# Projections of two batches from 49 products in two levels, with weight sums streamed from DRAM

## The chip, the cores and the metric

The kernel runs on one core of a Trainium2 chip. The metric is the device time of one execution in microseconds (us), as the median of several runs. All arithmetic is in fp32.

## What is computed

The input x is 64 batches of 256 nodes with 512 features, and a 256 x 256 adjacency matrix that all batches share. Two layers follow, each with a residual. Cut to what matters:

```python
h = relu(layernorm(x))                       # layer 0: graph attention
Wh = h @ W
logits = leaky_relu((Wh @ a_src)[:, :, None] + (Wh @ a_dst)[:, None, :], 0.2)
x = x + softmax(where(adj, logits, -inf)) @ Wh
h = relu(layernorm(x))                       # layer 1: 8 heads of 64
q, k, v = (split_heads(h @ M.T + b) for M, b in ((Wq, bq), (Wk, bk), (Wv, bv)))
a = softmax(where(adj, q @ k.T / 8, -inf)) @ v
x = x + merge_heads(a) @ Wo.T + bo
```

## The kernel before

**Tiling.** A group is one batch (GB = 1): 256 tokens in two halves of 128, 512 features in four chunks of 128. There are 64 groups. Each large product of 256 x 512 by 512 x 512 (or 256 x 256 by 256 x 512) is cut into two by two quarters and made from seven products of quarters in place of eight (a Strassen-Winograd form). `chained` (L624) holds it: seven terms, each a quarter or a sum of quarters of the left operand with a quarter or a sum of the right one. The products are summed in three PSUM banks, a, b and d: after every product the bank's running sum is read out and put, or added, to the quarters of the result that want it (`assemble`, L646).

**Stages.** In layer 0, `normalize0` (L960) makes h and the node terms, `weights0` (L1011) the edge weights em and the reciprocals rb of their sums, `quarters0` (L1057) scales em by rb and makes the sums of quarters of h and em on POOL, `aggregate0` (L1087) the product of em and h in 7 products of two 128-column matmuls, `transform0` (L1185) the product with W in 7 products of two 256-column matmuls, added to x. In layer 1, `normalize1` (L1192) and `transpose1` (L1220) make hT: VectorE transposes blocks of 32, and a trip through DRAM (z to rows to hT) does the rest. `project_qk` (L1263) makes queries and keys of one group in 7 products of eight 128-column matmuls, `project_v` (L1302) the values in 7 products of two 256-column matmuls. `attention` (L1325) makes the scores of four head pairs (arrays of 64 rows), exponentials on ScalarE, mask products and sums over the nodes on VectorE, the values product (arrays of 64 columns), and head sums `psm` in arrays of 32 columns (`head_sums`, L1373), whose reciprocal rc goes through DRAM to be spread over partitions (row, rb). `scale` (L1427) applies it; `output` (L1447) is the product with Wo in 7 products, added to x and stored. All weights and their sums lie in SBUF (`load_quarters`, L588; `combine_w`, L600).

**What sets the order.** The stages are generators. A list written out by hand (`first_half`, `second_half`) says in which order their steps are recorded. A planner (`Plan`) then orders the instructions: it gives each a duration (`cost`, L402), PE's steps a rank from the table `PHASE`, where one unit is one group, and plays the engines forward. PE takes the first step among the next AHEAD = 22 by rank that can start and for which PSUM banks are free; the other engines take what is due first. A chain of products reserves three of the eight banks. The order that comes out is issued as it stands, each engine a queue in order; SP issues nearly all DMAs. The planner's `Engine` issues everything, so the profile gives nearly every instruction the line L384; the tiles tell them apart.

**Names.** pqk_a, pqk_b, pqk_d: the banks of `project_qk`; pv: values; po: `transform0` with w_sb and `output` with wo_sb; pu: aggregate; psc: scores; pav: values product; psm: head sums; ps: edge sums; hs, us, as, hq, eq: sums of quarters; ex: exponentials; sm: their sums; va: values' left quarter, unpacked. The general path after the flag is not taken.

Of the kernel before, what the change touches and what calls it, by code (L numbers as in the profile page):

```python
# [30 lines left out]
class Buffer:  # L31

    def __init__(self, pool, shape, dtype, tag, name, bufs, real=None):
        self.pool, self.shape, self.dtype, self.tag, self.name = pool, shape, dtype, tag, name
        self.bufs, self.real = bufs, real
        self.grain = 32 if math.prod(shape[1:]) >= 256 else 1
        self.reads, self.writes, self.ops = [], [], []
        self.before = self.bank = self.chain = None

# [91 lines left out]
class Pool:  # L131
# [3 lines left out]
    def tile(self, shape, dtype, tag, name, bufs=None):  # L135
        base = Buffer(self.pool, shape, dtype, tag, name, bufs or self.bufs)
        made = self.made.setdefault(tag, [])
        if len(made) >= base.bufs:
            base.before = made[-base.bufs]
# [4 lines left out]
class Op:  # L144
# [12 lines left out]
AHEAD = 22  # L157
SLACK = 6.67358
SPARE = 1.08917
STEADY = 1  # L160
PHASE = {
    "aggregate0": [-1.42646, -1.3706, -1.36386, -1.35194, -1.33305, -1.33142, -1.3049, -1.30085],
    "attention": [0.44654, 0.6298, 0.47698, 0.36017, 0.40555, 1.35722],
    "output": [1.56205, 1.65037, 1.65572, 1.69495, 1.72281, 1.85231, 1.89845],
    "project_qk": [0.31881, 0.32614, 0.34745, 0.36874, 0.37077, 0.44626, 0.51693],
    "project_v": [0.62352, 0.64711, 0.66878, 0.71995, 0.81445, 0.83399, 0.9563],
    "transform0": [-0.55259, -0.50904, -0.48995, -0.48575, -0.45644, -0.44964, -0.39606],
    "weights0": [-1.61854, -1.58152, -1.43348],
}
8  # L170
# [3 lines left out]
class Plan:  # L174
# [16 lines left out]
    def record(self, engine, method, args, kwargs):  # L191
# [3 lines left out]
        for write, views in ((False, op.ins), (True, op.outs)):  # L195
            for v in views:
                base, bits = v.base, v.area()
                if write and base.before is not None:
                    for o in base.before.ops:
                        op.deps[o.at] = o  # L200
# [23 lines left out]
    def deadlines(self, slack):  # L224

        for n, block in enumerate(self.blocks):
            block.rank = n - len(self.blocks)
            if block.label is not None:
                stage, g, k = block.label
                block.rank = g + PHASE[stage][min(k, len(PHASE[stage]) - 1)]  # L230
# [18 lines left out]
    def schedule(self, ahead, slack):  # L249
# [60 lines left out]
        while len(order) < total:  # L310
# [12 lines left out]
            if free["tensor"] <= now:  # L323
                open_banks = [n for n, t in enumerate(bank_free) if t <= now]
                for n, block in enumerate(blocks[:ahead]):
# [11 lines left out]
                    for base in new.values():  # L337
                        if base.chain is not None:
                            if base.chain in reserved:
                                others -= reserved[base.chain]  # L340
                            else:
                                need = 3
                    if len(open_banks) < need + others:
                        continue
                    for base in new.values():
# [3 lines left out]
                        if base.chain is not None:  # L349
                            reserved[base.chain] = reserved.get(base.chain, 3) - 1  # L350
# [3 lines left out]
                    for op in block:  # L354
                        if op.kind != tile_kind:
                            t += 0.09 if tile_kind == (P, P) else 0.17
# [45 lines left out]
def cost(op):  # L402
# [15 lines left out]
    elif op.engine == "tensor":  # L418
        left = op.args[1]
        size = [next(s for s in (32, 64, 128) if k <= s) for k in (left.shape[0], left.size)]  # L420
        op.step = {512: 0.858, 256: 0.432, 128: 0.2245, 64: 0.24}.get(n, 0.11)
# [41 lines left out]
def kernel(  # L463
# [54 lines left out]
    half = const.tile([P, 2, Q], F32, tag="half", name="half")  # L518
    nc.gpsimd.memset(half, 0.0)
    for r in range(2):  # L520
        nc.gpsimd.memset(half[:, r, r * (Q // 2) : (r + 1) * (Q // 2)], 1.0)
# [44 lines left out]
    const_tiles = dict(ident=ident, ones=ones, half=half, minus_half=minus_half, bo_b=bo_b, flag=flag)  # L566

    def bounded(plan):
# [6 lines left out]
        ident, ones, half, minus_half, bo_b, flag = (  # L575
            plan.wrap(const_tiles[nm]) for nm in ("ident", "ones", "half", "minus_half", "bo_b", "flag")
# [44 lines left out]
        CHAIN = ((0, "a"), (2, "b"), (1, "a"), (4, "d"), (3, "a"), (6, "d"), (5, "a"))  # L621
        CHAIN_V = ((0, "a"), (1, "a"), (2, "b"), (4, "d"), (3, "a"), (6, "d"), (5, "a"))

        def chained(a, s, name, product, read, order=CHAIN):  # L624

            terms = (
                (partial(a, 0, 0), B11),
                (s[:, 1], T2),
                (partial(a, 0, 1), B21),
                (s[:, 2], T3),  # L630
                (s[:, 0], T1),
                (partial(a, 1, 1), T4N),
# [3 lines left out]
            for n, key in order:  # L636
                left, slot = terms[n]
                left = left() if callable(left) else left
                first = key not in banks
                if first:  # L640
                    banks[key] = bank([P, D], f"{name}_{key}", name)
                product(banks[key], left, slot, first)
# [20 lines left out]
        def product_rows(wt, dst, left, slot, first):  # L663
            for c in range(2):
                nc.tensor.matmul(
                    dst[:, 0:HD], left[:, c], wt[:, slot, c, :],
                    start=first and c == 0, stop=c == 1, skip_group_check=not first,
                )

        def product_cols(wts, dst, left, slot, first):  # L670
            for n, wt in enumerate(wts):
                for e in range(2):
                    at = (2 * n + e) * P
                    for c in range(2):
                        nc.tensor.matmul(
                            dst[:, at : at + P], wt[:, slot, c, e * P : (e + 1) * P], left[:, c],
                            start=first and at == 0 and c == 0, stop=c == 1,
                            skip_group_check=True,
                        )
# [16 lines left out]
        for i, tag in enumerate(("hT", "xn")):  # L696
            w_c.append(big.tile([P, 2, D], F32, tag=tag, name=f"w_{tag}", bufs=2 if tag == "hT" else 1))
# [6 lines left out]
        wq_sb = load_quarters(wqT, "wq_sb")  # L704
        wk_sb = load_quarters(wkT, "wk_sb")
        load_group(2)
        w_sb = load_quarters(w, "w_sb")
        wv_sb = load_quarters(wvT, "wv_sb")
# [4 lines left out]

# [60 lines left out]

        def whole(wt):

            return ((wt[:, B11], wt[:, T3]), (wt[:, B21], wt[:, B22]))
# [22 lines left out]
        def value_squares():  # L800

            for n, slot in enumerate((B11, B21, B22, T3)):
                junk = work.tile([P, DC // 2, HD], F32, tag="ex", name=f"junk_v_{n}", bufs=4)
                nc.scalar.activation(
                    junk, wv_sb[:, slot], AF.Square, accum_out=svs[:, n : n + 1]
                )
# [989 lines left out]
```

## Time and profile before

| what | value |
|---|---|
| median of 3 runs | 2823.18 us (2822.07 to 2823.32) |
| profiled execution, own time | 2824.94 us |
| its span, first to last instruction | 2823.2 us |
| mean granted TensorE clock | 0.999 |
| DMA | 184.49 MB, mean 65 GB/s |

The profile is one execution. PE is TensorE's matmuls, PEld its weight loads (beside PE), DVE VectorE, ACT ScalarE, POOL GpSimd, SP the engine that issues DMAs. A group row has the line, the engine, the operation, output and inputs by tile name, shapes, the count, then busy time and the mean of one, then the idle time of the engine just ahead of these instructions and what ended it. A timeline row has start and length in us, then the instructions merged. Ends of matmuls are modelled, so the pace is read from starts. An fp32 matmul leaves two records.

### The profile page before, as it was taken

The numbers are of one execution on the slowest core, as the hardware profiler recorded it, in microseconds if no ns is written. First come the engines' busy times: TensorE is split into PE (matmuls) and PEld (weight loads), VectorE is DVE, ScalarE is ACT, GpSimd is POOL, SyncE is SP. The second block draws the span as 40 slices with busy tenths as digits, with TensorE's granted clock in tenths as the row PEclk, the third lists the DMA queues.
The fourth block names the chain that finished last, engine by engine and source line by source line (L and its number), as shares of the span: only waits on it lengthen the run. The fifth ranks groups of instructions, "written<-read, shape, count | busy, mean of one in ns | idle before, by whom it ended". The sixth has DMA issues, their size and how long they took to land.

```text
span 2823.2 us, 52681 instructions
## 1 busy us (share of the span) xinstructions
PE 2799.1 (99%) x19698; PEld 2403.9 (85%) x19698; DVE 1838.9 (65%) x3314; ACT 1509.1 (53%) x3974; POOL 1528.7 (54%) x2020
## 2 busy tenths in 40 slices
PE   8999999999999999999999999999999999999999
PEld 5888888888888888888888888888888888888886
DVE  6776666666666666666666666665666666666654
ACT  5645655555555555555555555555555555555532
POOL 4645546556565555465565655554645656555540
PEclk9999999999999999999999999999999999999999
DMA  4022212122122222121221221211212212122120
GB/s 142 27 64 78 68 51 74 55 70 75 47 80 70 65 63 65 55 72 51 76 65 56 79 68 61 69 59 61 72 50 78 64 56 80 60 68 70 57 68 24
DMA packets 124074, 184.49 MB, mean 65 GB/s; under 512 B 28657, under 2 KB 74020, under 8 KB 123814
## 3 DMA queue, kind: packets, MB, share of 16 engines
q1 hardware_dynamic: 123718, 181.05, 20.4%
q8 instruction: 159, 2.61, 0.4%
q14 instruction: 101, 0.83, 0.1%
q0 software_dynamic: 96, 0.01, 0.0%
HBM read 106.44 MB, written 66.57 MB: 61 GB/s over the span
## 4 chain that ended last, share of the span: by engine, by line
PE 97%; ACT 1%; DVE 1%; DMA 0%; issue 0%; POOL 0%; SPq 0%; ACTq 0%
PE pqk_a L384 16%; PE po_a L384 15%; PE psc L384 9%; PE pqk_d L384 8%; PE pav L384 8%; PE pv_a L384 8%; PE po_d L384 8%; PE pqk_b L384 4%; PE pu_a L384 4%; PE pv_d L384 4%; PE po_b L384 4%; PE psm L384 2%; PE pv_b L384 2%; PE pu_d L384 2%; PE pu_b L384 1%; PE ps L384 1%
## 5 line engine op out<-in xcount | busy, mean ns | idle before, releaser
L384 DVE TENSOR_TENSOR ex<-ex,maskT 128x512 f32<-128x512 f32 x512 | 393.8, 800 | 95.0 <-ACT ex L384 95.0
L384 ACT ACTIVATE qk<-pqk_a,bias 128x128 f32<-128x128 f32 x756 | 221.1, 367 | 437.4 <-PE pqk_a L384 437.4
L384 POOL TENSOR_TENSOR em<-em,rb 128x256 f32<-128x256 f32 x122 | 120.1, 997 | 378.6 <-DVE rb L384 377.0
L384 ACT ACTIVATE ex<-psc 128x512 f32<-128x512 f32 x512 | 261.6, 617 | 117.0 <-PE psc L384 117.0
L384 POOL TENSOR_TENSOR as<-aT 128x256 f32<-128x256 f32 x62 | 64.7, 1044 | 423.2 <-PE pqk_a L384 271.0
L384 DVE TENSOR_TENSOR x<-po_a,x 128x256 f32<-128x256 f32 x500 | 205.1, 411 | 100.7 <-PE po_a L384 96.9
L384 PE MATMUL psc<-qk 64*128 64x256 f32 x2048 | 254.3, 389 | 2.1
L384 DVE SCALAR_TENSOR_TENSOR junk<-wa,h 128x512 f32<-128x512 f32 x252 | 183.3, 728 | 81.3 <-ACT h L384 76.6
L384 PE MATMUL pav<-ex,v 128*64 128x256 f32 x2048 | 236.0, 382 | 0.0
L384 DVE RECIPROCAL rc<-psm 128x256 f32<-128x256 f32 x64 | 112.4, 1756 | 185.9 <-PE psm L384 185.9
L384 PEld LDWEIGHTS psc<-qk 64*128 64x128 f32 x2048 | 187.2, 186 | 50.7 <-ACT qk L384 18.2
L384 DVE TENSOR_TENSOR sm<-ex 128x512 f32<-128x512 f32 x256 | 211.7, 828 | 0.0
L384 PEld LDWEIGHTS pav<-ex,v 128*64 128x64 f32 x2048 | 141.0, 137 | 81.8 <-issue 8.7
L384 POOL TENSOR_TENSOR x<-x,bo_b 128x512 f32<-128x512 f32 x128 | 172.2, 1358 | 63.7 <-ACT xn L384 61.5
L384 ACT ACTIVATE h<-x,nmr,rstd 128x512 f32<-128x512 f32 x128 | 101.1, 810 | 127.2 <-POOL nmr L384 127.2
L384 POOL TENSOR_TENSOR hq<-h 128x256 f32<-128x256 f32 x122 | 90.4, 742 | 122.3 <-PE pu_d L384 121.9
L384 ACT COPY v<-pv_a 128x256 f32<-128x256 f32 x192 | 70.6, 368 | 137.8 <-PE pv_a L384 134.8
L384 POOL TENSOR_TENSOR hs<-hT 128x256 f32<-128x256 f32 x128 | 100.4, 806 | 75.0 <-PE pv_d L384 64.2
L384 POOL TENSOR_TENSOR us<-uT 128x256 f32<-128x256 f32 x126 | 106.8, 866 | 61.9 <-DVE uT L384 61.8
L384 PE MATMUL pqk_d<-hs,wq_sb 128*128 128x128 f32 x1008 | 135.4, 277 | 0.0
L384 PE MATMUL po_a<-w_sb,uT 128*128 128x256 f32 x504 | 133.7, 388 | 0.5 <-DVE x L384 0.5
L384 PE MATMUL pqk_a<-hs,wq_sb 128*128 128x128 f32 x1008 | 133.2, 275 | 0.0
(229 smaller groups left out, 7373.4 us busy)
## 6 DMA issues: line engine op xcount, KB each, us to landing
x<-in_x_dram SPq DMA_DIRECT2D x64, 512.0 KB
out_dram<-x SPq DMA_DIRECT2D x128, 256.0 KB
rows<-z SPq DMA_DIRECT2D x62, 512.0 KB
hT<-rows SPq DMA_DIRECT2D x248, 128.0 KB
rb<-row SPq DMA_DIRECT2D x124, 256.0 KB
es_b<-es_b SPq DMA_DIRECT2D x61, 127.0 KB
row<-rc SPq DMA_DIRECT2D x124, 4.0 KB
es_b<-es SPq DMA_DIRECT2D x122, 0.5 KB
```

Of the source, the lines that this page charges most:

```text
L384: getattr(getattr(self.nc, op.engine), op.method)(*map(real, op.args), **{k: real(a) for k, a in op.kwargs.items()})
```

## The change

**Projections.** `project_qk` and `project_v` go; `project(g)` makes queries, keys and values of two groups, g and g + 1, together. The left operand is now 512 tokens by 512 features, cut two by two with one group as each row of quarters, and each of the 7 products of this level is again made from 7: 49 products, each of a 128 x 256 by 256 x 128 shape with its inner 256 in two slots. Their matmuls are three of 128 columns for queries, keys and values. In the outer level the sums of the left operand, S, are made on POOL; in the inner level their halves' sums are made on VectorE (`half_sums`). After each of the 49 products a read of 384 columns (three times 128) takes the bank's running sum: eight are copies with bias on ScalarE, 41 are adds on VectorE into a tile `total` or one of four result tiles c; two sums of such tiles (`add_up`) are on POOL.

**Weight sums from DRAM.** The 49 right operands no longer fit: `weight_products` makes them during the first pair (subtractions on VectorE, copies on ScalarE) into chunks, which are used and stored to a DRAM tensor `products`. Each later pair loads them again in 28 DMAs of up to 128 x 768 values, through four buffers `wst`, on SP.

**Chains.** All chains use two banks, a and b; product 4 starts bank b anew. A chain reserves two banks in the planner.

**Reciprocals.** In `weights0` the edge sums come out with one column a half (`ps` of 128 x 2), their reciprocal is of two columns, two transposes spread it over 256 columns of PSUM (`prs`), and VectorE scales em by it, a step that POOL did in `quarters0`. In `head_sums`, for all but the last two groups, the 256 columns are folded into 64: 32 matmuls of 64 columns with `eighths` in place of 8 of 256, then a reciprocal of 64 columns and three DMAs in place of four.

**Order.** The hand-written list goes. Stages are recorded pair after pair, each score step, values step and head sum a step of its own, and the table `PHASE` has one row for even and one for odd groups, interpolated over a stage's steps (STEPS); AHEAD is 9. The unit is still one group. hT is unpacked by ScalarE into `left` in one copy a half, so `va` goes. The first group is projected through the same 49 products as the others.

The core of the diff:

```diff
-AHEAD = 22
-SLACK = 6.67358
+AHEAD = 9
+SLACK = 3.38563
+STEPS = {"project": 49, "transform0": 7, "output": 7, "aggregate0": 8}
 PHASE = {
+    "project0": [-0.08576, 0.2165, 0.52314, 0.90716, 1.04988, 1.47497, 1.83359, 2.09944],
+    "attention0": [0.75994, 0.85786, 1.51533, 1.51841, 1.68258, 1.67665, 1.79903],
+    "attention1": [2.13243, 2.11902, 2.3234, 2.30657, 2.53841, 2.54761, 2.50817],
+    "output0": [2.11483, 2.51629, 2.65299],
+    "output1": [3.16977, 3.36346, 3.50541],
+    "weights00": [-1.67184],
...
-                                need = 3
+                                need = 2
...
-        CHAIN = ((0, "a"), (2, "b"), (1, "a"), (4, "d"), (3, "a"), (6, "d"), (5, "a"))
+        CHAIN = ((0, "a"), (2, "b"), (1, "a"), (4, "b"), (3, "a"), (6, "b"), (5, "a"))
+        FIRST = (0, 2, 4)
...
+            sums(nc.gpsimd, [S[:, m] for m in range(4)], a)
+            for n in ORDER:
+                if n in groups:
+                    x, name, members = groups[n]
+                    s = half_sums(x, name)
...
+                for slots in CHUNKS:
+                    chunk = chunk_of(f"wst_{g}_{n}_{slots[0]}")
...
+                    if g == 0:
+                        weight_products(n, chunks, slots)
+                        both = both[1], both[0]
+                    nc.sync.dma_start(*both)
+                banks = {}
+                for l, key in CHAIN:
+                    if key not in banks:
+                        banks[key] = bank([P, D], f"pp_{g}_{n}_{key}", f"pp_{g}_{n}")
+                    ps, first = banks[key], l in FIRST
+                    for m in range(3):
+                        pair = chunks[l][:, m], terms[l]
+                        nc.tensor.matmul(
+                            ps[:, m * P : (m + 1) * P], *(pair if m < 2 else reversed(pair)),
+                            start=first and m == 0, stop=True, skip_group_check=True,
                         )
+                    read(n, l, ps)
+                    yield
...
+            if g:
+                prs = bank([P, N], f"prs_{g}")
+                for t in range(NT):
+                    nc.tensor.transpose(
+                        prs[:, t * P : (t + 1) * P], rs[:, t : t + 1].to_broadcast([P, P]), ident
+                    )
+                nc.vector.tensor_mul(em, em, prs.unsqueeze(1).to_broadcast([P, NC, N]))
...
-                for m in range(NC):
-                    nc.gpsimd.tensor_tensor(em[:, m, :], em[:, m, :], rb, op=ALU.mult)
...
+                psm = bank([P, N // parts], f"psm_{g}")
+                rc = work.tile([P, N // parts], F32, tag="rc", name=f"rc_{g}")
                 for r in range(2):
+                    for c in range(parts):
+                        at = Q - (parts * r + c + 1) * (Q // (2 * parts))
+                        for e in range(DC):
+                            nc.tensor.matmul(
+                                psm[e * Q : (e + 1) * Q, :],
+                                ones_at[:, at : at + Q],
+                                sums[e][:, r, c * (N // parts) : (c + 1) * (N // parts)],
+                                start=(r == 0 and c == 0),
+                                stop=(r == 1 and c == parts - 1),
+                            )
                 nc.vector.reciprocal(rc, psm)
```

## The prediction

> **What bounds the kernel now.** I read the page's head and the chain that ended last first: they say which engine sets the end.
>
> ```profile
> span 2823.2 us, 52681 instructions
> ## 1 busy us (share of the span) xinstructions
> PE 2799.1 (99%) x19698; PEld 2403.9 (85%) x19698; DVE 1838.9 (65%) x3314; ACT 1509.1 (53%) x3974; POOL 1528.7 (54%) x2020
> ...
> PE 97%; ACT 1%; DVE 1%; DMA 0%; issue 0%; POOL 0%; SPq 0%; ACTq 0%
> ```
>
> TensorE is busy 99% of the span and carries 97% of the chain. A busy PE isn't yet a PE at its peak, so I read the windows next, over nine groups at a time (columns: length, then busy time and instructions of each engine).
>
> ```profile
> 541.20:930.30 389.10, 388.77 (x2756) 337.28 (x2756) 254.52 (x460) 211.54 (x558) 217.12 (x288) 1.00 0.21 65
> 930.30:1319.40 389.10, 388.77 (x2756) 337.27 (x2755) 254.60 (x460) 211.53 (x558) 217.11 (x288) 1.00 0.21 65
> ```
>
> The two stretches are alike: 389.1/9 = 43.23 us a group, DVE 28.3, ACT 23.5, POOL 24.1 of it. Two groups, a pair, cost 86.5 us. Then the timeline of PE, for the pace (from one start to the next; every fp32 matmul leaves two records).
>
> ```profile
> 1428.99 1.03 PE L384 MATMUL pv_a<-wv_sb,va 128*128 128x256 f32 x4
> 1429.95 3.67 PE L384 MATMUL pav<-ex,v 128*64 128x256 f32 x32
> 1433.55 1.07 PE L384 MATMUL psm<-sm,half 128*32 128x256 f32 x16
> 1434.55 1.13 PE L384 MATMUL po_a<-w_sb,uT 128*128 128x256 f32 x4
> 1435.52 1.03 PE L384 MATMUL po_b<-w_sb,uT 128*128 128x256 f32 x4
> 1436.38 1.03 PE L384 MATMUL po_d<-w_sb,us 128*128 128x256 f32 x4
> ...
> 1443.41 1.05 PE L384 MATMUL pqk_a<-hs,wq_sb 128*128 128x128 f32 x8
> 1444.30 1.06 PE L384 MATMUL pqk_a<-hs,wk_sb 128*128 128x128 f32 x8
> ```
>
> Eight records of 128 columns take 0.893 us (0.2233 a matmul), four of 256 take 0.864 (0.432 a matmul): 1.69 to 1.74 ns a column, so a saved column is saved time. A change of array shape costs 0.10 going in and up to 0.20 coming out (psm to po_a to po_b: 0.14 + 0.10 over the bare pace). A group is 56 matmuls of 128 for queries and keys (12.50), 14 of 256 for values (6.05), 28 for the two transforms (12.10), 14 of 128 for the aggregate (3.11), scores and values 3.46 each, head sums 0.86, edge sums 0.43: 41.97. The remaining 1.25 us are shape changes, three visits to the narrow shapes a group. No wait is left in it.
>
> **What the Trainium skill says.** "TensorE: Matmul & The Clock Gate", section "Back-to-back issue gap", gives matmuls of 1 to 64 columns a floor of about 25 ns each. The trace before has 64-column work only in the Gram products, at (23.17 to 24.16)/32 = 31 ns a record with the shape change in it: it shows nothing faster, though there only two array parts work side by side and streaming alone would give 27. "TensorEngine Tiling (Array Packing)", section "Key Properties", says that a change of tiling mode drains the array; the 0.10 to 0.20 us above agree. "SBUF — State Buffer", section "Who interferes with whom", says that a DVE instruction with two SBUF inputs contends with a POOL instruction that reads SBUF, one with a single SBUF input doesn't. The trace agrees: the mask product (two SBUF inputs) runs 648 to 1694 ns, the add from PSUM of po_d 405 to 426.
>
> **The change, part by part, for a pair.** The rows of DVE that the costs come from:
>
> ```profile
> L384 DVE TENSOR_TENSOR x<-po_d,x 128x256 f32<-128x256 f32 x250 | 104.7, 419 | 36.0 <-PE po_d L384 33.7
> L384 DVE TENSOR_TENSOR qk<-qk,pqk_b 128x512 f32<-128x512 f32 x63 | 43.3, 687 | 100.6 <-PE pqk_b L384 84.3 <-ACT qk L384 16.3
> L384 DVE RECIPROCAL rc<-psm 128x256 f32<-128x256 f32 x64 | 112.4, 1756 | 185.9 <-PE psm L384 185.9
> L384 DVE RECIPROCAL rb<-rb 128x256 f32<-128x256 f32 x63 | 110.0, 1745 | 0.7
> ```
>
> *Products, on the path.* Out: 2 x (12.50 + 6.05) = 37.1 us. In: 49 x 3 = 147 matmuls of 128 columns x 0.2233 = 32.8. **-4.3 us.** This is the one gain on PE.
>
> *Edge sums, on the path.* Out: one 256-column product a group, 0.432. In: the one-column form that group 0 uses now (four records from 34.60 to 34.97, 0.37) and two transposes (eight of them from 88.65 to 89.52, 0.109 each): 0.59. **+0.3.**
>
> *Head sums, on the path.* 8 matmuls of 256 become 32 of 64 columns. The streamed columns are the same (0.86 us); at the Gram pace of 27 ns, 64 records take 1.73. The truth lies between, 0 to +0.87 a group; no gain is possible, as no column is saved. Weight loads of two array parts overlap in the Gram products (a 64-column load shows 53 ns less than a 128-column one, yet records come every 27 to 31), so I expect overlap with four parts too and take 1.1 us: **+0.5** (0 to +1.7).
>
> *Order of PE, on the path.* Scores now get a step for each head pair and the values and head sums steps of their own. I sorted the steps of one steady pair by the new planner ranks: 107 steps with 11 separate visits to narrow shapes, against six a pair now. The planner skips steps that can't start, so some will merge. 11 x 0.39 = 4.3 against 2.5: +1.8 at most, +0.6 if they merge to 8. I take **+1.5** (0.6 to 2.2).
>
> *DVE, beside PE.* Added: 41 adds of 384 columns out of PSUM, between the 419 and 687 ns rows at 0.55, 0.47 in a row as they overlap by 0.08: 19.3. Half sums, 12 of 256 and four of 128 columns: 4.9, with 2.4 for the port (0.15 each, about what the mask product loses now). The scaling of em, moved here from POOL, 2 x 0.61. Removed: adds to qk and v 5.7; the reciprocal of rb with the clamp ahead of it shrinks from 256 columns to two, -3.5; rc from 256 to 64 columns, -2.4. Sum 56.6 + 16.2 = 72.8 us of a pair, 86%. It stays under PE's 84.5, but the cover shrinks from 30 us to 12. ACT loses 2 x 7 us of copies and gains 24 small ones and the unpacking of hT, POOL trades hs and em x rb for the S sums and add_up (768 columns, about 1.8 us each): both stay below 60%, at no cost.
>
> *Waits added.* With two PSUM banks a chain, product l + 2 waits for the read of product l. DVE's queue stands between: adds and masks of 0.4 to 0.8 us. The ranks spread the 49 steps over 2.19 groups, one each 1.9 us, which leaves 3 us for a read; and free banks rise, as a chain needs two, not three. I take **+0.3** for reads that come late (0 to 1.5).
>
> *Weight sums from DRAM.* 128 x 49 x 384 x 4 B = 9.63 MB a pair, in 28 issues on SP. The hardware queue moved 181.05 MB in 20.4% of the span: 314 GB/s, so 30.7 us; DMA goes from 21% to about 58%. A chunk of 393 KB takes 1.3 us and serves 1.3 us of PE spread over 3, and four buffers cover some 9 us. 28 x 0.36 us of issue come to SP's 11 us (30 issues a pair); the copy of rc takes three DMAs a group in place of four. Behind a chunk that waits for its buffer stand es_b, rows, hT and rb, and behind those the exponentials, the S sums and the scaling. I take 0, up to +1 if the queue blocks.
>
> *The ends.* Group 0 gives up its plain projections: 19.9 against 18.55, a further -1.3 - but the first pair makes its weight sums: 56 subtractions and two sets of sums, 24 us of DVE, of which 13 were there as combine_w. Filling reaches 5.2 groups from first step to last, against 3.5 now, and the last pair's projections have no next layer-0 work beside them. PE idle at the ends is 24 us now; I add **+20** (5 to 45).
>
> Sum: -4.3 + 0.3 + 0.5 + 1.5 + 0.3 = -1.7 us a pair, x 32 = -54; ends -1 + 20: **-35**. The profiled execution has 2823.2 us in its span and 2824.9 in all; the median of the runs is 2823.2, so 1.7 lower. Against the median: 2788; I say **2790**.
>
> **Rivals.** *All of it is kept* (merged visits, head sums at the column pace): -4.3 + 0.3 + 0.6 = -3.4 x 32 + 5 = -105, about 2720 to 2750. For it: PE shows no wait now and the planner can fill well; against: the ranks. *The gain is eaten on PE* by visits and short matmuls: 0.3 + 1.7 + 2.2 against -4.3 is -0.1 a pair, with ends 2820 to 2840. *DVE takes over, slower*: at 86% any further delay, above all port waits (by their shortest durations, the DVE instructions with two SBUF inputs, 32 us a pair, and POOL's, 43 us, fill 75 of 84), makes reads late, the two-bank chains stop, and PE idles. It is slower from the point where DVE needs over 86.5 us a pair, 13.7 above my sum, a further 0.25 us on each of some 54 contended instructions; at 88 us with the ends: 2870. For it: single masks take up to 1.7 us; against: the mean now is 0.8. *The stream comes late, slower*: SP, one queue for everything, stands behind a chunk and the next hT or chunk is late. Each us that PE loses so a pair is +32; at 3 us: 2880. Against it: DMA at 58%.
>
> **How the numbers follow.** Forecast near 2790 (2760 to 2812) 0.52; all kept 0.13; eaten 0.15, half of it under 2817; DVE 0.15; stream 0.05. 0.2% of the time is 5.6 us, about what a measurement of this kernel can tell from no change. Faster: 0.52 + 0.13 + 0.03 = 0.68; same 0.09; slower 0.23. The range leaves a tenth out on each side: 2740 to 2862.
>
> **What would show it.** PE busy 98% or more and a steady pair of 84 to 85.5 us; psm with 64 records in 0.9 to 1.7 us; DVE 83 to 90%; DMA about 0.55; 10 or so narrow visits a pair. Wrong it would be if PE waits on DVE for the total or c tiles by over 2 us a pair, if chunks keep PE waiting, or if the first and last 100 us lose over 45.

## The result and the profile after

The changed kernel takes 2911.28 us (median, 2907.17 to 2912.62), against 2822.62 of the kernel before in the same session: a ratio of 1.031 (1.029 to 1.033), 3.1% slower. The forecast was 2790, within 2740 to 2862.

The head of the page and the chain that ended last, of the changed kernel:

```profile
span 2910.7 us, 63452 instructions
...
PE 2784.8 (96%) x23422; PEld 2386.9 (82%) x23422; DVE 2473.6 (85%) x4865; ACT 1361.5 (47%) x3454; POOL 1713.8 (59%) x1903
...
PE 71%; DMA 15%; DVE 7%; ACT 3%; issue 2%; POOL 1%; SPq 0%; ACTq 0%; DVEq 0%; POOLq 0%
PE pp_a L399 15%; PE po_a L399 12%; PE pp_b L399 11%; DMA es_b<-es_b 9%; PE pav L399 8%; PE po_b L399 7%; PE psc L399 6%; DMA wst<-products 5%; PE pu_a L399 3%; PE pu_b L399 3%; PE psm L399 2%; DVE ex L399 2%; ACT e L399 2%; DVE c L399 1%; DVE e L399 1%
```

TensorE carried 97% of the chain before and carries 71% now. Of the rest DMA has 15, and two transfers hold nearly all of it: the weight chunks `wst`, which are new, and `es_b`, which is not. The latter spreads a group's 256 source scores over 127 partitions, from a row that lies in partition 0, and stands in both kernels alike. In the lines of the changed kernel pp_a and pp_b are the two banks of `project`, tt is its `total`, c its result tiles, sa to sd the half sums, left the unpacked hT, e the edge terms that ScalarE makes from es_b. The windows, over the same two stretches as before:

```profile
541.20:930.30 389.10, 378.28 (x3236) 328.75 (x3233) 335.40 (x661) 179.11 (x456) 239.81 (x264) 1.00 0.58 173
930.30:1319.40 389.10, 379.02 (x3240) 326.87 (x3240) 336.91 (x660) 188.73 (x472) 241.44 (x271) 1.00 0.58 175
```

VectorE at 86% and DMA at 0.58 are the shares that were forecast. TensorE is idle 10 to 11 us of 389 where it had been idle 0.3.

**Where the time went.** I took every PE record's start in the trace, from one to the next, and subtracted the bare pace of its kind; what is over at a change of array shape and just after it counts as shape change, any other excess of more than 0.15 us as a stop. The 27 pairs between the 7th and the 61st head sums give, in us a pair:

| kernel | pair | PE work | shape changes (visits) | stops |
|---|---|---|---|---|
| before | 86.46 | 83.98 | 2.49 (5.3) | 0 |
| changed, as forecast | 84.75 | 80.5 | 4.0 (about 10) | 0.3 |
| changed, measured | 88.14 | 80.06 | 4.66 (9.0) | 3.42 |

The stops are 1.29 ahead of the first chain that reads the half sums `sc`, 0.68 ahead of `sa`, 0.60 ahead of `sb`, 0.34 ahead of an output chain, 0.28 ahead of `sd` and 0.23 at others (most of it ahead of `left`). For the whole span, 87.5 us longer: 32 pairs at +1.68 make +54, so the ends make +34.

### The profile page after: what moved, and what is told of

It reads as the page before. It is cut to its first block, busy times and chain, and to the rows that moved or that the text cites. A ratio compares the mean times of both kernels' runs of the same rounds, so it can differ in the third digit from the quotient of the medians.

```text
span 2910.7 us, 63452 instructions
## 1 busy us (share of the span) xinstructions
PE 2784.8 (96%) x23422; PEld 2386.9 (82%) x23422; DVE 2473.6 (85%) x4865; ACT 1361.5 (47%) x3454; POOL 1713.8 (59%) x1903
## 4 chain that ended last, share of the span: by engine, by line
PE 71%; DMA 15%; DVE 7%; ACT 3%; issue 2%; POOL 1%; SPq 0%; ACTq 0%; DVEq 0%; POOLq 0%
PE pp_a L399 15%; PE po_a L399 12%; PE pp_b L399 11%; DMA es_b<-es_b 9%; PE pav L399 8%; PE po_b L399 7%; PE psc L399 6%; DMA wst<-products 5%; PE pu_a L399 3%; PE pu_b L399 3%; PE psm L399 2%; DVE ex L399 2%; ACT e L399 2%; DVE c L399 1%; DVE e L399 1%
## 5 line engine op out<-in xcount | busy, mean ns | idle before, releaser
L399 POOL TENSOR_TENSOR c<-tt,c 128x768 f32<-128x768 f32 x128 | 246.4, 1934 | 168.7 <-DVE c L399 102.6
L399 PE MATMUL psc<-c 64*128 64x256 f32 x2048 | 274.6, 397 | 0.0
L399 PE MATMUL pav<-ex,c 128*64 128x256 f32 x2048 | 236.5, 382 | 0.0
L399 PEld LDWEIGHTS psc<-c 64*128 64x128 f32 x2048 | 182.9, 187 | 44.2 <-DVE z L399 8.6
L399 PEld LDWEIGHTS pav<-ex,c 128*64 128x64 f32 x2048 | 141.1, 137 | 79.5 <-issue 10.5
L399 DVE TENSOR_TENSOR tt<-tt,pp_a 128x384 f32<-128x384 f32 x288 | 157.6, 547 | 42.4 <-PE pp_a L399 39.9
L399 DVE TENSOR_TENSOR c<-c,pp_b 128x384 f32<-128x384 f32 x288 | 157.4, 547 | 36.2 <-PE pp_b L399 31.4
L399 DVE TENSOR_TENSOR x<-po_b,x 128x256 f32<-128x256 f32 x375 | 153.0, 409 | 33.2 <-PE po_b L399 32.9
L399 PE MATMUL pp_a<-S,wst 128*128 128x128 f32 x1024 | 157.8, 277 | 7.5 <-POOL S L399 4.1
L399 PEld LDWEIGHTS pp_a<-S,wst 128*128 128x128 f32 x1024 | 142.8, 193 | 14.2 <-POOL S L399 4.3
```

The lines of the kernel that those rows point to most:

```text
L399: getattr(getattr(self.nc, op.engine), op.method)(*map(real, op.args), **{k: real(a) for k, a in op.kwargs.items()})
```

## The experiments

Two theories stood against each other. The transfer theory (A): the `es_b` broadcast is slow, a weight chunk or the exponentials wait behind it, and PE behind those. The VectorE theory (B): VectorE is too full, or its port too contended, and the two-bank chains' reads are late. The expectations name a third (C): the stream of weight chunks is too much as such. The table of waits (us in total, times, longest) names both, with the one that ACT's exponentials `e` have; changed kernel first, kernel before second:

```profile
ACT e L399 <- DMA es_b<-es_b: 68.3, 44, 7.3
...
PE pp_a L399 <- DVE c L399: 36.7, 31, 3.0
...
PE pp_a L399 <- ACT tt L399: 16.5, 28, 1.7
PE pp_a L399 <- DMA wst<-products: 16.0, 31, 1.2
```

```profile
ACT e L384 <- DMA es_b<-es_b: 4.6, 4, 3.5
```

About one stop of each kind a pair: a read by VectorE (`sc`), a read by ScalarE (`sa`), a chunk (`sb`). ACT waited for `es_b` 4 times before and waits 44 times now. The critical chain of a pair in the middle shows how they hang together (start, length, what):

```profile
1396.96 0.88 PE pp_b L399 x6
1397.85 0.33 SPq L399
...
1398.27 8.36 DMA es_b<-es_b
...
1406.73 0.51 ACT e L399
...
1408.53 0.66 ACT tt L399 x3
...
1409.24 0.94 PE pp_a L399 x6
...
1434.68 6.53 DMA wst<-products
```

The broadcast takes 8.36 us. ACT stands at `e` until it is there; its next work is the copy of a bank into `tt`, and PE's next product waits for that bank. The first two lines say why the broadcast starts there: SP had to issue a weight chunk ahead of it, which waited for products in pp_b to free its buffer. A chunk stands straight ahead of 58 of the 61 broadcasts in SP's queue, and a broadcast is issued on average 3.4 us after the last write to its row has been, where the kernel before has 1.5. 26 us later a chunk takes 6.5 us, where the median chunk takes 3.1. SP's own timeline shows what was issued ahead of it, the next broadcast:

```profile
1432.45 0.68 SPq L399 DMA_DIRECT2D es_b<-es_b  x1
1434.68 0.33 SPq L399 DMA_DIRECT2D wst<-products  x1
```

and one window just after the broadcast was issued (length, engines, granted clock, DMA share, GB/s):

```profile
1433.40:1434.60 1.20, 1.20 (x12) 1.12 (x12) 1.20 (x4) 0.00 (x0) 1.20 (x3) 1.00 0.06 20
```

A share of 0.06 is one DMA engine of 16: all 127 rows go through one. The packets in the trace agree: 127 packets of 1 KB start one after the other, nearly all 42 ns apart, from 1433.77 to 1439.44. Of the 128 packets of 3 KB of the chunk behind it, 120 start by 1437.2, which is the share of fifteen engines at eight each; the chunk is complete at 1441.2, 8.8 us after the broadcast's issue. The trace doesn't number the engines, so that the last eight waited for that one is inferred from these counts.

The experiments e1 to e6, e9 and e10 are edits of the changed kernel, and each engine keeps the planner's order of it; e7 and e8 are edits of the kernel before.

**e1, the broadcast out of a row in DRAM.** The two copies of `es` go to a row in DRAM, and from there to all 128 partitions.

```diff
-                    nc.sync.dma_start(es_b[0:1, t * P : (t + 1) * P], es[:, t : t + 1])
+                            lambda ap, t=t: es_row(g)[0:1, t * P : (t + 1) * P]
...
-                            tensor=ap.tensor, offset=ap.offset, ap=[ap.ap[0], [0, P - 1], [1, TOK]]
+                            tensor=es_row(g).tensor, offset=es_row(g).offset,
+                            ap=[[0, P], [1, TOK]],
```

> The broadcast of es over partitions (es_b, 127 rows, 7.5 to 8.4 us from issue to the end of the wait in the chain) is replaced by one over 128 rows from a row in DRAM, with the planned order of every engine kept as it is; a matter of the same bytes. Theory A (this one transfer, which runs long by itself and which the weight chunks queue behind, makes ACT's exponentials and then the chunks late): es_b lands in under 4.5 us, the stops of PE ahead of the sa and sb products (0.68 + 0.60 us a pair) go, and the time falls by 30 to 70 us, to 2840 to 2880. Theory B (VectorE, 86% busy, reads the chains late): within 6 us of 2911. Theory C (the stream of weight sums as such is too much for the DMA engines): within 6 us of 2911.

Measured: 3392.0 us, a ratio of 1.201 (1.198 to 1.204). A miss, and not by the broadcast, which now takes 4.9 us. The writes of 128 single values to DRAM stand out (the DMA issues: KB each, median us to landing; then SP's own waits):

```profile
es_row<-es SPq DMA_DIRECT2D x122, 0.5 KB, 11.8
```

```profile
SPq L399 <- DMA es_row<-es: 436.3, 62, 12.7
```

The same values into SBUF landed in 2.5 us. SP stands for 436 us in all until these writes have landed, before it can issue the broadcast, and with it all that its queue holds behind. Transfers that are issued are late too: rb takes 9.4 us where it took 4.5. The stops grow to some 20 us a pair. So the edit exchanged one slow transfer for two slower ones. It says nothing on the gain that A expected. It shows that a slow transfer on this queue delays what comes after it, but largely by another way than in the changed kernel: here SP itself waits for a landing.

**e2, the mask product on 64 of 512 columns.** Leaves most of the mask out.

```diff
-                    nc.vector.tensor_mul(ex[:, r, :, :], ex[:, r, :, :], maskT)
+                    nc.vector.tensor_mul(
+                        *(v.then(lambda ap: ap[:, :, 0:32]) for v in (ex[:, r], ex[:, r], maskT))
+                    )
```

> The mask product of the scores is done on 64 of 512 columns of each tile, the rest is left unmasked (part of the computation is left out); order of every engine kept. This takes some 7 us a pair and 16 uses of the shared port from VectorE. Theory B: PE's stop ahead of the sc product (1.29 us a pair) and those behind other late reads go, 35 to 70 us less, 2840 to 2875. Theory A and C: at most 15 us less, as the waits for DMA stay.

Measured: 2893.69 us (2885.85 to 2895.06), 1.026 (1.024 to 1.027). VectorE falls from 85% to 76% of the span, and the gain is 18 us, a little over the 15 that A allowed and half of what B asked for. The stop ahead of `sc` shrinks from 1.29 to 0.86 us a pair; those ahead of `sa` and `sb` stay at 0.60 and 0.56. VectorE's load is not the cause of most of it.

**e3, chunks of 32 columns.** The loads stay, of 32 columns each into the same buffers; the products use old values. Leaves nearly all of the weight stream out.

```diff
+                    else:
+                        both = tuple(v.then(lambda ap: ap[:, 0:32]) for v in both)
                     nc.sync.dma_start(*both)
```

> From the second pair on each chunk of weight sums loads only 32 of its 384 or 768 columns per row, the rest keeps older values (part of the computation is left out); the same count of DMAs in the same order, es_b as in the changed kernel. DMA share falls from 0.58 to under 0.35. Theory C: stops go, 40 us less or more, 2870 or below. Theory A: es_b still takes 8 us, so ACT's wait stays; only the chunk behind it is a matter of its 4 us more, so between 5 and 25 us less. Theory B: within 6 us of 2911.

Measured: 2861.44 us (2857.78 to 2862.07), 1.014 (1.012 to 1.016): 50 us less. The stops ahead of `sa`, `sb` and `left` are gone (0.02 us together); the one ahead of `sc` is untouched, 1.29, and PE's wait for DVE c still 36.5 us. So there are two causes, and the stream has a part in one. 50 us is what C expected (40 or more), and A expected 5 to 25. Whether the stream costs this by itself or only with what shares its queue is for e5 to say, which leaves the stream whole.

**e4, e1 and e2 together.**

> The es broadcast over 128 rows and the narrowed mask product (64 of 512 columns, the rest unmasked, part of the computation left out) together, order kept. If A and B are both at work the two gains add, 2780 to 2830, and a steady pair comes to 84.5 to 85.5 us, the sum of products and shape changes; if only one is, this is within 8 us of the better of the two alone.

Measured: 3380.64 us, 1.199 (1.197 to 1.201), 11 less than e1 alone, within the spread of the two kernels' runs. The slow writes hide what else it might have told.

**e5, the broadcast in two parts.** 127 rows become 112 and 15.

```diff
+                plan.ops[-1].cuts = (P - Q // 2, Q // 2 - 1)
...
+                for n in op.cuts:
+                    self.nc.sync.dma_start(
+                        to[at : at + n],
+                        bass.AP(
+                            tensor=row.tensor, offset=row.offset, ap=[row.ap[0], [0, n], row.ap[-1]]
+                        ),
+                    )
+                    at += n
```

> The es broadcast over 127 rows (one transfer, 8.2 us) is cut into two transfers of 112 and 15 rows from the same row in the same place; nothing else is changed, and every engine keeps its order. Theory A (a transfer of 127 rows runs on one DMA engine and takes 8 us, and chunks that were issued behind it have to wait for that engine): es_b lands in 3 to 4 us, the stops of PE ahead of the sa, sb and left products (1.5 us a pair) go as they did with the narrow stream, and the time falls by 35 to 55 us, to 2856 to 2876. Rival C (the stream as such, 58% of the DMA engines, makes everything late): at most 10 us less, since the bytes are the same.

Measured: 2872.36 us (2870.16 to 2873.72), 1.017 (1.016 to 1.019): 39 us less with one DMA more a group. Waits of the two kinds in this kernel:

```profile
ACT e L412 <- DMA es_b<-es_b: 29.6, 15, 6.3
...
PE pp_a L412 <- DMA wst<-products: 6.0, 10, 1.3
```

ACT's wait that is put down to `es_b` falls from 68 to 30 us; a further 14 us ahead of `e` are now put down to chunks, so ACT's whole idle time there, under any name, falls from 99 to 54. PE's wait for chunks falls from 16 to 6; the stop ahead of `sa` goes from 0.68 to 0.03, `sb` from 0.60 to 0.28, and the broadcast, 9% of the chain before, isn't among its larger parts. `sc` keeps 1.34. The stream is whole, so C, which allowed 10 us, is out. This fits the Trainium skill, "DMA: Bandwidth & Descriptors": its section "Why a DMA increments its semaphore by 16 and not by 1" says that a DMA uses the largest number of engines up to 16 that divides its outer dimension, so one for 127 and 16 for 112, and "Queues, rings and completion order" that each engine takes a queue's descriptors in the order of its ring. The trace of the changed kernel agrees: 0.06 of the engines just after the issue, 8.4 us, and a chunk behind it that takes 6.5.

The landing itself was a miss. I expected 3 to 4 us; the two parts take 6.5 and 6.0:

```profile
es_b<-es_b SPq DMA_DIRECT2D x61, 112.0 KB, 6.5
es_b<-es_b SPq DMA_DIRECT2D x61, 15.0 KB, 6.0
```

Chunks issued 1.5 to 5 us behind a broadcast take 5.5 us on average here and 6.5 in the changed kernel, against 3.1 to 3.5 for those issued over 12 us behind one (chunks whose landing the trace has). So the cut takes about one us off the chunk and one to two off the broadcast. That is more than the stops were long (0.6 to 0.7 us a pair), but it doesn't clear the queue. Why the parts still take over 6 us, no run here shows.

**e6, GpSimd's additions in halves.** `add_up` adds 768 columns in one instruction; now two of 384 follow each other.

```diff
+                    plan.ops[-1].parts = 2
...
+            for n in range(op.parts):
+                args = [a[:, n : n + 1] for a in args]
```

The reason was the other stop in the chain. The timeline of POOL and of DVE in the changed kernel, ahead of one `sc` stop that ends at 1451.8:

```profile
1446.72 4.03 POOL L399 TENSOR_TENSOR c<-tt,c 128x768 f32<-128x768 f32 x2 [3.90 <-DVE c L399]
```

```profile
1446.83 2.25 DVE L399 TENSOR_TENSOR e<-e,e 128x512 f32<-128x512 f32 x1
...
1449.67 1.63 DVE L399 TENSOR_TENSOR ex<-ex,maskT 128x512 f32<-128x512 f32 x1
1451.23 0.54 DVE L399 TENSOR_TENSOR c<-c,pp_a 128x384 f32<-128x384 f32 x1
```

Two additions in a row hold POOL from 1446.7 to 1450.75. VectorE's sum `e`, 0.69 us at the median, ends only after the first of them; its mask product, 0.68 at the median, ends 0.55 after the second. The read of the bank, `c<-c,pp_a`, stands behind both, and PE behind that. "SBUF — State Buffer", section "Who interferes with whom", says that a VectorE instruction with two SBUF inputs contends with a GpSimd instruction that reads SBUF, and calls the port pair that they share an exclusive lock; the lengths here agree with it.

> POOL's add of two quarter tiles (768 columns, 1.93 us) is issued as two adds of 384 columns; same work, same order. Theory D (PE's stop ahead of the sc product, 1.29 us a pair, comes from VectorE instructions that wait out POOL's long add for the shared port): the stop shrinks by half or more, 15 to 30 us less. Rival B (VectorE is late by its own work): within 6 us of 2911, or up to 8 more for POOL's 64 x 4 extra instructions.

Measured: 2879.02 us (2872.76 to 2881.06), 1.020 (1.019 to 1.022): 32 less, a little over the 15 to 30 expected. An addition takes 1.08 us in place of 1.93, POOL in all 22 us more. PE's wait:

```profile
PE pp_a L404 <- DVE c L404: 5.9, 5, 3.8
```

36.7 us became 5.9; the `sc` stop is gone, `sa` and `sb` stay at 0.62 and 0.61. The mirror image of e5. The longest `e` is 1.44 us where it was 2.25, and VectorE, with the same instructions, is busy 33 us less, as it should be if the two share a port. But the cut changes a second thing. Around the same read of this pair POOL's pieces no longer form one block:

```profile
1424.15 1.17 POOL L404 TENSOR_TENSOR c<-tt,c 128x384 f32<-128x384 f32 x1
1428.05 1.00 POOL L404 TENSOR_TENSOR c<-tt,c 128x384 f32<-128x384 f32 x1 [2.73 <-DVE c L404]
1429.74 2.40 POOL L404 TENSOR_TENSOR c<-tt,c 128x384 f32<-128x384 f32 x2 [0.69 <-ACT c L404]
```

A piece can start as soon as its own inputs are there. How much of the 32 us comes from shorter holds of the port and how much from the spread, e6 can't tell.

**e7, two-bank chains in the kernel before.** This part of the change alone; the planner orders the program anew, with the old ranks.

```diff
-        CHAIN = ((0, "a"), (2, "b"), (1, "a"), (4, "d"), (3, "a"), (6, "d"), (5, "a"))
+        CHAIN = ((0, "a"), (2, "b"), (1, "a"), (4, "b"), (3, "a"), (6, "b"), (5, "a"))
+        FIRST = (0, 2, 4)
...
-                                need = 3
+                                need = 2
```

> One part alone, on the kernel before: all chains in two PSUM banks, two reserved by the planner. If the two-bank chains are what lets a late read stop PE: slower by 10 to 60 us. If they cost nothing with VectorE at 65% (the prediction): within 8 us of 2822.

Measured: 2869.79 us (2869.34 to 2873.53), 1.017 (1.016 to 1.019): 48 us more, within the first case and not the prediction's. A pair costs 87.80, +1.34, of which 0.75 lies ahead of the scores, which come sooner after the reads of queries and keys (PE waits 25.1 us in 50 pieces for ACT's copies qk). Two banks aren't free under ranks that were made for three. How much is the chains and how much the other order, it can't tell.

**e8, the reciprocals' part in the kernel before.** `weights0`, `head_sums` and the DMAs of rc as in the change, nothing else; the planner orders anew.

```diff
-                psm = bank([P, N], f"psm_{g}")
+                psm = bank([P, N // parts], f"psm_{g}")
...
-                for m in range(NC):
-                    nc.gpsimd.tensor_tensor(em[:, m, :], em[:, m, :], rb, op=ALU.mult)
+                nc.vector.tensor_mul(em, em, prs.unsqueeze(1).to_broadcast([P, NC, N]))
```

> One part alone, on the kernel before: edge sums in one column a half with the transposes and VectorE's scaling of em, head sums folded into 64 columns. By the prediction's prices PE pays 0.3 us a pair (+10 us) and VectorE falls by 4 us a pair to about 60%. If the new chain of edge sums (sum, reciprocal, transposes, scaling) makes the aggregate late under the old ranks: slower by 20 to 60 us, with PE waiting for rs or em.

Measured: 2835.9 us (2834.33 to 2838.25), 1.0045 (1.003 to 1.006). VectorE falls from 65% to 59%, and the time rises by 14, near the 10 of the prediction's prices: VectorE wasn't the bound. PE work rises by 0.36 us a pair (edge sums and transposes), shape changes fall as the order merges visits (4.0 a pair): a pair costs 0.12 more, 4 us over 32 pairs, and the ends the rest.

**e9, both repairs.** e5 and e6 in the changed kernel.

> The changed kernel with both repairs at once: the 127-row broadcast of the source scores cut into 112 and 15 rows, and GpSimd's 768-column additions issued as two of 384; the order of every engine is unchanged. If the two causes are independent (the broadcast, worth 39 us alone; the long additions, 32 us alone), the time is 2840 us (2833 to 2850), a ratio of 1.006, and of the stops ahead of a chain, sc, sa and sb together, less than 0.6 us a pair of groups is left where the changed kernel has 2.6. If both repairs free the same slack (what is late next after one of them is what the other frees), it stays at 2855 to 2872 us. The rival that the stops aren't what counts, and that VectorE's load of 86 per cent is, has no gain over the better of the two: 2870 us.

Measured: 2835.72 us (2832.22 to 2839.48), 1.004 (1.003 to 1.006): 76 us less than the changed kernel, against 39 + 32 = 71. The two gains add, and stops are down from 3.42 to 0.98 a pair. VectorE is still at 86% of the span. A pair costs 85.54 now, 0.92 less than before; the ends, +44 by the account above, keep the kernel slower.

**e10, the first pair's weight sums off VectorE.** e9 with 56 subtractions made copies on ScalarE. Leaves the subtractions out.

```diff
+                    if l in (1, 3, 4, 5):
+                        plan.ops[-1].as_copy = True
...
+            if op.as_copy:
+                self.nc.scalar.copy(*map(real, op.args[:2]))
+                continue
```

This is about the ends. The windows from 60 to 120 us, changed kernel and kernel before:

```profile
60.00:120.00 60.00, 43.37 (x277) 36.36 (x276) 49.89 (x109) 30.35 (x102) 35.24 (x32) 0.86 0.27 101
```

```profile
60.00:120.00 60.00, 59.32 (x401) 49.25 (x401) 46.15 (x78) 39.21 (x113) 40.88 (x45) 1.00 0.08 25
```

PE is idle 17 of 60 us and the granted clock is 0.86. The first head sums come at 156 us, where they came at 114.

> The changed kernel with both repairs, and the 56 subtractions of the first pair's weight sums made plain copies on ScalarE; the order of every engine is otherwise unchanged. This leaves the subtractions out (the keys, queries and values of every group are other numbers), and takes 34 us from VectorE before 220 us and gives ScalarE some 17 us. If VectorE's weight sums are what makes the start long (the first head sums begin at 157 us where the kernel before has 114), the start shortens by 20 to 40 us: first head sums at 115 to 137 us, the whole 2797 to 2815 us, and the half-granted stretches of the clock before 150 us get fewer. The rival, that the start is long because the order has the first pair's edges, additions of activations and loads of weights late, whatever VectorE does, has the first head sums at 150 us or later and a time of 2826 to 2836 us.

Measured: 2840.42 us (2835.31 to 2841.62), 1.006 (1.005 to 1.008); the first head sums at 158. No gain: the 34 us of VectorE's weight sums don't set the start. That rules the first case out; it doesn't show the rival's own cause, the order.

**e11, new ranks with both repairs.** The table of ranks searched anew against the planner's own length, with offsets for the first three and last two pairs; AHEAD (now 13), SLACK and two more numbers of the planner changed with it, and the additions are recorded as pieces of 384.

```diff
-                for t in range(2):
-                    nc.gpsimd.tensor_tensor(
-                        to[:, 2 * t : 2 * t + 2], x[:, 2 * t : 2 * t + 2], y[:, 2 * t : 2 * t + 2],
+                for t in range(4):
+                    nc.gpsimd.tensor_tensor(to[:, at], x[:, at], y[:, at], op=ALU.add)
...
+                block.rank += SHIFT.get(g // 2, {}).get(f"{stage}{g % 2}", 0.0)
```

> The changed kernel with both repairs (the broadcast in 112 and 15 rows, the additions on GpSimd in pieces of 384 columns, here known to the planner), and with the table of ranks searched anew; the first three and the last two pairs have offsets of their own. Nothing is left out of the computation. The planner's own length of the program falls from 2851.6 us (the order of the changed kernel) to 2793.0. The kernel with both repairs took 2835.7 in the old order. If it is the order that costs the start and the rest of the middle, about that difference comes off: 2777 to 2800 us, faster than the kernel before. If the start is long because the first product needs two batches and the loads and sums ahead of it, whatever the order, the first head sums still begin after 150 us and what is left is the middle's share: 2810 to 2835 us.

Measured: 2801.12 us (2800.47 to 2804.24), 0.992 (0.991 to 0.994): 0.8% less than the kernel before, 3.8% less than the changed one. Span, busy times and the chain:

```profile
span 2802.5 us, 63579 instructions
...
PE 2755.8 (98%) x23422; PEld 2380.2 (85%) x23422; DVE 2454.9 (88%) x4865; ACT 1362.3 (49%) x3454; POOL 1724.8 (62%) x2031
...
PE 94%; DVE 2%; issue 2%; DMA 1%; ACT 1%; POOL 0%; SPq 0%; DVEq 0%; POOLq 0%; ACTq 0%
```

VectorE is fuller than in the slow kernel, the chain is TensorE's again, and stops are 0.27 us a pair. A pair takes 84.97: 79.93 of PE work, 4.77 of shape changes in 11 visits, near the forecast's row of the table. Against e9 the middle gives 15 us of the 35, the first three pairs 19. The first head sums come at 147 us, still 33 after the kernel before: neither expectation had this mixture right.

**e12, the same with the broadcast whole.**

```diff
-                plan.ops[-1].cuts = (P - Q // 2, Q // 2 - 1)
```

> The kernel with the new ranks and the additions in pieces, but with the broadcast of 127 rows in one transfer as the change has it; same order on every engine. If the cost of the one transfer belongs to the transfer and not to one particular order, it is 25 to 50 us slower than the same order with the broadcast in two parts (39 us was measured in the old order, 43 with the additions already in pieces), and chunks and exponentials wait for es_b again. If only the old order happened to have it in a tight place, the difference is less than 15 us.

Measured: 2836.77 us (2832.73 to 2837.97), 1.0045 (1.003 to 1.006): 36 us more than e11.

```profile
ACT e L420 <- DMA es_b<-es_b: 92.5, 59, 7.0
```

The cost goes with the transfer, not with one order. It stops other chains in this order (`sa` 0.52, `left` 0.49), and costs about the same.

## Why the prediction was wrong

The forecast was a gain of 35 us; the loss is 88. Of these 123 us, the stops are 100 (3.42 us a pair against +0.3), shape changes 21 and the ends 15, less 13 that PE's work gained. The steps that failed are the two that priced the stops. By the prediction's own steps, for a pair:

- *Products*, -4.3, *edge sums*, +0.3, *head sums*, +0.5: -3.5 in all, measured -3.92 of PE work. The head sums cost nothing, as the timeline of PE shows:

```profile
1420.72 1.10 PE L399 MATMUL psm<-sm,eighths 128*32 128x64 f32 x64
1421.75 0.71 PE L399 MATMUL pp_a<-sa,wst 128*128 128x128 f32 x4
```

  From start to start 1.03 us, 0.14 of it the shape change: 0.89 for 64 records, the streamed columns' own time (0.86). That is 13.9 ns a record, 27.8 for an fp32 matmul with its two records. The Trainium skill ("TensorE: Matmul & The Clock Gate", section "Back-to-back issue gap") gives a floor of about 25 ns; read for a record, as I read it, it doesn't hold here, where four array parts work side by side. Read for a whole matmul, these runs don't contradict it.
- *Order of PE*, +1.5: nine visits where I counted eleven and expected some to merge, but at 0.52 us each and not 0.39: +2.2, at the end of the range. The mechanism was right, the price of a visit too low.
- *DVE*, 86%: it is 86% in the windows, and that is luck. The sum was 72.8 us of a pair of 84.5; measured are 76.0 of 88.14, 3.2 more work in a longer pair. The rival "DVE takes over" (2870) has the direction, and mostly for the wrong reason. VectorE's load isn't what stops PE: e2 takes a tenth of it away for 18 us, e11 runs at 88% with 0.27 us of stops a pair. What it has right is the port, in one place: GpSimd's two additions ahead of one read a pair (e6).
- ***Waits added*, +0.3, is the first step that failed.** I took the mean lengths of VectorE's queue, 0.4 to 0.8 us, against 3 us for a read. The read ahead of `sc` stands behind a sum and a mask product of 2.25 and 1.63 us, since two 1.93-us additions run on POOL beside them: 1.29 us a pair, 32 us in the end (e6). That is four times the +0.3, though still within the 0 to 1.5 that I gave. I had listed "about 1.8 us each" for these additions and priced them at nothing, as POOL is below 60%. The price of a long POOL instruction isn't POOL's time, but what it does to VectorE beside it.
- ***Weight sums from DRAM*, 0, is the second.** I reckoned with bytes (58% of the engines: right) and with the queue's issues, and asked what stands behind a chunk that waits. That path is there: the broadcast is issued 3.4 us after its row is written and not 1.5, since a chunk stands ahead of it. But e5 leaves this delay at 3.3 us and takes the stop ahead of `sa` away, so the delay alone doesn't stop PE. What I left out is the other way round: the chunk stands behind the broadcast, on the one engine that the broadcast uses. The stops ahead of `sa`, `sb` and `left` came to 1.5 us a pair, where I had 0 and at most +1. The planner couldn't see it either: `cost` books 127 x 0.25 / 16 = 2.0 us for it, as if all engines took part. The row was in the kernel before, where only 4.6 us of waits were on it; I take it that nothing that PE needed soon was behind it, which no run tried. The change put 28 chunks a pair on that queue, and the broadcast in one piece came to cost 39 us (e5), 36 in another order (e12). The rival "the stream comes late" named the result, +32 for each us a pair, but as SP's queue and at a chance of 0.05; none of the rivals had the length of a transfer that was already there.
- *The ends*, +19: +34 for the changed kernel, by the same account, within the 5 to 45 given. The last pairs are 21 us shorter than before, the first three 64 longer; 8 of the difference are the five pairs' share at 1.68. VectorE's sums aren't the cause (e10), new ranks take a part (e11). In the changed kernel products that need no S start at 56.9 us; those that read S start only after the second group's normalization and POOL's sums. The kernel before has its plain products from 48 us on (critical chains, changed kernel first):

```profile
73.02 4.39 POOL S L399 x3
77.46 1.65 PE pp_a L399 x6
```

```profile
48.43 10.63 PE pqk L384 x48
```

  That the first pair's dependence on two groups sets the rest of the start is my reading; no run tried it.
- *The chances* don't add up as written: half of the 0.15 for "eaten" is 0.075, not the 0.03 that "faster" counts.

Of the signs of being wrong that I had named, chunks did keep PE waiting (16 us). PE's waits for c and tt came to 1.3 us a pair, under the 2 that I named, and were still worth 32 us (e6).

So the sum should have been -3.9 + 2.2 + 3.4 = +1.7 a pair, x 32 = +54, and +34 of ends: 88. With both stops repaired and new ranks the forecast's steady pair (84.75) is nearly reached, 84.97, and the kernel is at 2801.

Open: the cost of two-bank chains by themselves in the changed kernel's order, and what of e7's 48 us is order; what of e6's gain is the port; why a chunk behind the cut broadcast still takes 5.5 us; and the rest of the start.

## What to carry to other kernels

When a change adds transfers to a queue, look at every transfer that is already on it, for its length and for how many DMA engines it uses, also where hardly a wait shows today: here 127 rows went through one engine, and cutting them into 112 and 15 was worth 36 to 39 us. When a change adds long GpSimd instructions, look at which reads of VectorE can fall behind one, and try it in pieces; the share of busy time tells nothing of it. An engine at 88% need not be the bound: test it by taking work from it before believing it.

## What the runs showed of the hardware

- A broadcast of 127 rows of 1 KB from one partition takes 8.2 to 8.4 us in the pair shown and keeps one of 16 DMA engines busy (share 0.06, 20 GB/s, a packet every 42 ns); a 384-KB load issued 2.2 us behind it takes 6.5 us in place of 3.1. Cut into 112 and 15 rows (e5) it lands in 6.5 and 6.0 us.
- 128 values of 4 bytes written to DRAM take 11.8 us, to SBUF 2.5.
- 64-column fp32 matmuls in arrays of 32 columns, four side by side, run at 13.9 ns a record, two records a matmul.
- Two GpSimd additions of 384 columns take 2.17 us, one of 768 takes 1.93: 12% more on POOL for 32 us less in all. Beside the long additions a VectorE sum of 0.69 us took up to 2.25, beside the short ones up to 1.44 (e6).
